# Channel attention on one core: a third buffer for its rows in lent memory, four band buffers, two staging buffers, and one DMA for the rows at a strip edge

## Chip, cores and metric

The kernel runs on one NeuronCore of a Trainium2 chip, in float32 but for one late stage. The metric is the device time of one launch in microseconds (us). The kernel before has a median of 4351.41 us over three runs (4345.83 to 4355.03).

## The reference, cut to what matters

Two layers follow each other on an image batch of shape 4 x 192 x 128 x 128. The first is channel attention with 8 heads of 24 channels, the second a dilated neighbourhood attention. The change lies in the first.

```
# layer 0
qkv = dwconv3x3(conv1x1(x, w_qkv), w_dw)         # 768 channels, 3x3 depthwise, SAME
q, k, v, l = split(qkv, 4)                        # 192 channels each
q, k, v = heads(q), heads(k), heads(v)            # [B, 8, 24, H*W]
q = q / max(norm(q), 1e-12); k likewise           # over all pixels
attn = softmax(einsum("bhcn,bhdn->bhcd", q, k) * temperature)
out = einsum("bhcd,bhdn->bhcn", attn, v)
L = silu(fc2(relu(fc1(mean(l, pixels)))))         # one gate per channel
x = conv1x1(L + out + x, w_proj) + L
# layer 1
x = x + dwconv3x3(x, pos_w) + pos_b
q, k, v = conv1x1(x, qkv_w); attention over 3x3 windows with dilation 1, 2, 3
out = conv1x1(concat, proj_w)
```

## The kernel before, in words

Three stages run one after the other.

`project` (0 to about 820 us) reads x in 64 groups of four rows, multiplies by the 1x1 weights, stores the products for q and k in the DRAM tensor `qk_dram` (laid out row, channel, image, column), and convolves v on DVE, POOL and ACT into `v_dram` and `v2_dram`. A planner (`Schedule`, line 38, wrapped by `Stage`) puts its instructions in order by hand-given costs and places (`PLACES1`), all engines, SP's DMA issues too. Column and row sums for the gate are kept in tiles of `gate_p` (`xsum`, `xcol`, `xrow`, two of each).

`channel_attention` (line 658, about 820 to 1569 us) loops over 8 heads. In each it convolves 24 channels of q and 24 of k on the tensor engine (PE), and forms the products q k^T of each image. Image rows lie on partitions. A 3x3 depthwise convolution becomes, for each column shift dx, a matmul with a banded 32 x 32 matrix over rows; PE is used as sixteen tiles of 32 x 32 (L720), so 24 matmuls make one channel of all four images (6 PSUM buffers `pc`). The work of a head is cut into six turns of 8 channels: q and k, each with j = 0, 2, 4. For each turn `loaded` (L687)
- loads a staging tile `few` of 96 KB with the band's entries (L691, one buffer),
- loads the rows `u` of the 8 channels, 2 MB, by 7 DMAs (L703; the four groups of strips are rotated against each other, so one group takes one DMA and three take two); the pool `u_p` has two buffers,
- builds the turn's band on POOL: four copies of 32 x 720 (L710) and eight of 32 x 6 (L712), into one of two bands, `bands[turn % 2]`.

`evicted` moves a channel from PSUM on ACT (L729) and takes its statistics on DVE (L731). Strips of 32 rows lack the taps that cross their edges. For these, three times a head, `cut_loaded` (L752) loads the four rows around an edge for q and for k (L759: eight DMAs of 48 KB), `cut_convolved` (L766) runs 12 matmuls `pcut` on them after channels 14, 30 and 46, and `cut_turned` (L787) transposes the result (after channels 18 and 34, and inside the gram). `products` (L802) makes the gram of a head, 256 matmuls of 128 x 96 (L807), and small matmuls `sm` (L827 to L845). `finish` (L853) is a generator whose pieces run in the next head after every fourth channel: softmax, two groups of `pm` matmuls with the output weights, and four stores into the tiles `mix1` and `mix2` on SP (L887, L890).

The order on PE is the order of the program text (`manual_schedule(engines={PE})`, L938), with the column shifts of neighbouring channels interleaved. The order on the other engines, SP's queue among them, is set by the framework's scheduler. All of this stage's DMAs are issued by SP, in one queue, and an issue waits there until its target buffer is free.

`second_pass` (L945, 1569 to 4348 us) does layer 1 with the planner again, one iteration per group of four rows of an image pair, 64 in all, about 42.5 us each. Its inputs come in `xv` tiles of 128 x 512 (`loads`, L985; L993 and L996), six per iteration, from a pool `p2xv` of eight buffers that exists from the kernel's start (L337). The products `ph` (L1006) read them. The planner takes the number of buffers from `XV = 8` (`hold`).

The change touches `channel_attention_then_dilated_attention`, `channel_attention`, and in it `loaded`, `cut_loaded`, `products` and `finish`.

Of the kernel before, what the change touches and what calls it, by code (L numbers as in the profile page):

```python
# [7 lines left out]
F32 = mybir.dt.float32  # L8
# [5 lines left out]
B, C, H, W = 4, 192, 128, 128  # L14
HEADS0 = 8
# [22 lines left out]
class Schedule:  # L38
# [6 lines left out]
    def __init__(self, change, change_rank):  # L45
        self.ops, self.pools = [], {}
        self.change, self.change_rank = change, change_rank
# [86 lines left out]
def reached(n, dy):  # L134

    p, i = divmod(n, NB)
    rows = [i * RB + o + dy for o in range(RB)]
    return {p * NB + (-r if r < 0 else 2 * (H - 1) - r if r >= H else r) // RB for r in rows if -4 < r < H + 3}


class Stage:
# [172 lines left out]
@with_exitstack  # L314
def channel_attention_then_dilated_attention(ctx: ExitStack, tc: tile.TileContext, d, out: bass.AP):
    nc = tc.nc
    x = d["x"]
    const = ctx.enter_context(tc.tile_pool(name="const", bufs=1))
    dram = ctx.enter_context(tc.tile_pool(name="dram", bufs=1, space=bass.MemoryType.DRAM))

    def load(pool, name):
        t = pool.tile(list(d[name].shape), d[name].dtype, tag=name, name=name)
        nc.sync.dma_start(t, d[name])
        return t

    mix1, mix2, biases = [], [], []
    for b in range(B):
        mix1.append(const.tile([128, C], F32, tag=f"mix1{b}", name=f"mix1{b}"))
        mix2.append(const.tile([128, C], F32, tag=f"mix2{b}", name=f"mix2{b}"))
    for p in range(B // 2):  # L330
        biases.append(const.tile([128, NG], F32, tag=f"bias{p}", name=f"bias{p}"))
    qk_dram = dram.tile([H, 2 * C, B, W], F32, tag="qk_dram", name="qk_dram")
    v_dram = dram.tile([B // 2, 128, H, 2, W], F32, tag="v_dram", name="v_dram")
    v2_dram = dram.tile([B, G, H, W], F32, tag="v2_dram", name="v2_dram")


    wts2, xv_p = (ctx.enter_context(tc.tile_pool(name=n, bufs=k)) for n, k in (("p2w", 1), ("p2xv", XV)))  # L337
    with ExitStack() as early:
        band_p, u_p = (early.enter_context(tc.tile_pool(name=n, bufs=k)) for n, k in (("pab", 1), ("pau", 2)))
        gate_w = early.enter_context(tc.tile_pool(name="p1g", bufs=1))  # L340
        gate_p = early.enter_context(tc.tile_pool(name="p1s", bufs=2))
        sums = []
        for p in range(B // 2):
            xsum = gate_p.tile([128, 3, NB], F32, tag="xsum", name=f"xsum{p}")
            xcol = gate_p.tile([128, 3, 2, H], F32, tag="xcol", name=f"xcol{p}")
            xrow = gate_p.tile([128, 3, 3], F32, tag="xrow", name=f"xrow{p}")
            nc.gpsimd.memset(xrow, 0.0)
            sums.append((xsum, xcol, xrow))
        later = {}

        def load_later(name, pool):
            later[name] = load(pool, name)

        def load_mix(b):
            nc.sync.dma_start(mix2[b][0:G], d["wp2"])

        loads = [(load_later, n, gate_w) for n in GATE] + [(load_later, n, wts2) for n in SECOND]
        loads += [(load_mix, b) for b in range(B)]
        project(tc, x, load, loads, sums, qk_dram, v_dram, v2_dram)
        gates = [  # L360
            lambda ps, p=p: gate_bias(nc, gate_p, ps, p, *sums[p], *(later[n] for n in GATE), biases[p])
            for p in range(B // 2)
        ]
        channel_attention(tc, d, load, qk_dram, mix1, mix2, band_p, u_p, gates)
        w2 = {n: later[n] for n in SECOND}
    second_pass(tc, x, w2, xv_p, mix1, mix2, biases, v_dram, v2_dram, out)


def project(tc, x, load, other_loads, sums, qk_dram, v_dram, v2_dram):
# [285 lines left out]
    nc.vector.tensor_copy(bias, pb)  # L655


def channel_attention(tc, d, load, qk_dram, mix1, mix2, band_p, u_p, gates):

# [4 lines left out]
    with ExitStack() as ctx:  # L666
# [1 line left out]
        k_p = ctx.enter_context(tc.tile_pool(name="pak", bufs=1))  # L668
        wts = ctx.enter_context(tc.tile_pool(name="paw", bufs=1))
        cut_p = ctx.enter_context(tc.tile_pool(name="pac", bufs=1))  # L670
        few_p = ctx.enter_context(tc.tile_pool(name="pax", bufs=1))
        st = ctx.enter_context(tc.tile_pool(name="pas", bufs=1))
        fin = ctx.enter_context(tc.tile_pool(name="paf", bufs=1))
        ps_c = ctx.enter_context(tc.tile_pool(name="papc", bufs=6, space=bass.MemoryType.PSUM))
# [3 lines left out]
        bands = [band_p.tile([128, 4, 2, 3, STRIP], F32, tag=f"band{k}", name=f"band{k}") for k in range(2)]  # L678
        for band in bands:
            nc.gpsimd.memset(band, 0.0)  # L680
        logits = fin.tile([CH0, B, HEADS0, CH0], F32, tag="logits", name="logits")
        nq = fin.tile([CH0, B, HEADS0], F32, tag="nq", name="nq")
        nk = fin.tile([CH0, B, HEADS0, CH0], F32, tag="nk", name="nk")
        def shifted(dx):
            return slice(max(0, 1 - dx), min(W, W + 1 - dx)), slice(max(0, dx - 1), min(W, W + dx - 1))

        def loaded(hd, which, j):  # L687
# [5 lines left out]
                d["bands"][:, which * C + hd * CH0 : which * C + (hd + 1) * CH0]  # L693
                .rearrange("p (e c) x m -> p e (c x m)", e=4)[:, :, j * 3 * STRIP : (j + 2) * 3 * STRIP],
            )
            u = u_p.tile([128, 4, 2, B * W], F32, tag="u", name=f"u{which}_{hd}_{j}")
            for e in range(4):
                turn = e * STRIP
                for to, of in ((slice(turn, 128), slice(0, 128 - turn)), (slice(0, turn), slice(128 - turn, 128))):
                    if of.start == of.stop:  # L700
                        continue
                    first = c0 + e * (CH0 // 4)
                    nc.sync.dma_start(  # L703
                        u[to, e].rearrange("p c w -> p (c w)"),
                        qk_dram[of, first : first + 2].rearrange("h c b w -> h (c b w)"),
                    )
            band = bands[(3 * (2 * hd + which) + j // 2) % 2]
            for i in range(4):
                group = slice(i * STRIP, (i + 1) * STRIP)
                nc.gpsimd.tensor_copy(band[group, :, :, :, 1 : STRIP - 1], few[:, :, :, :, 1 : STRIP - 1])  # L710
# [41 lines left out]
        def cut_loaded(hd, edge):  # L752
            us = []
            for which in range(2):
                c0 = which * C + hd * CH0
                u = cut_p.tile([4 * CH0, B * W], F32, tag=f"u{which}", name=f"cut{which}_{hd}_{edge}")
                first = (edge + 1) * STRIP - 2
                for r in range(4):
                    nc.sync.dma_start(  # L759
                        u[r * CH0 : (r + 1) * CH0],  # L760
                        qk_dram[first + r, c0 : c0 + CH0].rearrange("c b w -> c (b w)"),
                    )
                us.append(u)
            return us

# [36 lines left out]
        def products(hd, q, sq, k, sk, cuts, s_cut):  # L802
# [43 lines left out]
                    sm[:, 2 * B * CH0 + b : 2 * B * CH0 + b + 1], sq[:, b, :], ones[:, :1], start=True, stop=True  # L846
                )
            by_image = lambda a: a.rearrange("p (b c) -> p b c", b=B)
            nc.vector.tensor_copy(logits[:, :, hd, :], by_image(sm[:, : B * CH0]))
            nc.vector.tensor_copy(nk[:, :, hd, :], by_image(sm[:, B * CH0 : 2 * B * CH0]))  # L850
            nc.vector.tensor_copy(nq[:, :, hd], sm[:, 2 * B * CH0 : EXTRA])

        def finish(hd):  # L853


            rows, norm_q, norm_k = logits[:, :, hd, :], nq[:, :, hd], nk[:, :, hd, :]
            wide = lambda a: a.unsqueeze(2).to_broadcast([CH0, B, CH0])
            for a in (norm_q, norm_k):
                nc.scalar.activation(a, a, AF.Sqrt)
# [18 lines left out]
            for b in range(0, B, 2):  # L878
# [1 line left out]
                pm = ps_g.tile([HALF, B, HALF], F32, tag="gram", name=f"pm{hd}_{b}")  # L880
                two = pm.rearrange("p b c -> p (b c)")[:CH0].rearrange("p (h o) -> p h o", h=2)
                for e in range(2):
                    nc.tensor.matmul(two[:, e, :], logits[:, b + e, hd, :], wph[:, hd, :], start=True, stop=True)
                nc.vector.tensor_copy(mixed, two)
                for e in range(2):
                    if low:
# [694 lines left out]
```

## Time and profile before

| what | value |
|---|---|
| median of three runs | 4351.41 us |
| the profiled execution's own time | 4350.1 us |
| its span, first to last instruction | 4348.2 us |
| granted PE clock, mean | 0.984 |
| busy: PE, DVE, POOL, ACT | 4178.9, 3833.7, 3411.2, 2633.4 us |
| DMA | 676.91 MB, mean 156 GB/s |
| channel attention (820 to 1569 us): PE, DVE, ACT, POOL busy | 689.1, 453.6, 293.9, 236.8 of 749 us |
| its DMA share and rate | 0.63, 160 GB/s |
| projection (100 to 820 us): PE busy, DMA share, rate | 715.1 of 720 us, 0.84, 263 GB/s |
| second pass (1700 to 4000 us): PE, DVE, POOL busy | 2277.7, 2262.1, 2162.8 of 2300 us |
| head 5 (1299 to 1389 us): bytes moved | 14.77 MB |
| head 5: DMA issues on SP | 42 of `u`, 24 of `cut`, 6 of `few`, 2 of `cuttaps`, 4 of `mix` |

Such a page is read like this. "Busy" is time in which an engine executed something; on PE that includes time in which only one of sixteen tiles is at work. The chain of waits is followed back from the last instruction to what released it, step by step. In the table of waits, "A <- B" is time in which engine A stood still with its next instruction at line A, and B came last of what it needed. SPq is the queue of SP: a DMA that stands there holds all behind it.

### The profile page before, as it was taken

The page shows a single profiled execution, that of the slowest core. Times are in us where ns is not written, and L with a number is a line of the kernel's source. Part 1 is how long each engine was busy: PE and PEld are TensorE (multiplying, and loading weights), DVE is VectorE, ACT ScalarE, POOL GpSimd, SP SyncE. Part 2 cuts the span into 40 slices and gives each one's busy share as a digit, 9 for nine tenths or more (in the row PEclk, how much of TensorE's full clock was granted, in tenths as well). Part 3 has the DMA queues.
Part 4 walks back from the last instruction along what each step waited for, and adds up shares of the span by engine and source line. Part 5 has one row for each costly group of instructions (what it writes and reads, how often), then busy time and mean ns, then how long its engine had stood idle before and what let it go on. Part 6 is the DMA issues. An engine that isn't in the chain of part 4 may idle for free.

```text
span 4348.2 us, 74751 instructions
## 1 busy us (share of the span) xinstructions
PE 4178.9 (96%) x25728; PEld 1655.8 (38%) x25728; DVE 3833.7 (88%) x5572; ACT 2633.4 (61%) x4906; POOL 3411.2 (78%) x3409
## 2 busy tenths in 40 slices
PE   8999999899999989999999999999999999999996
PEld 3333333355565543333333333333333333333331
DVE  6999999865656647999999999999999999999996
ACT  6999999733334347565566555665656556566531
POOL 6888888633323315999999999999999999999998
PEclk9999999899999999999999999999999999999997
DMA  8888888766656647566665676656656666665521
GB/s 253 266 267 255 267 273 265 216 168 167 173 137 168 169 109 156 128 135 130 126 129 129 133 130 126 137 116 133 130 126 134 128 129 130 131 136 124 115 50 32
DMA packets 478219, 676.91 MB, mean 156 GB/s; under 512 B 138048, under 2 KB 313612, under 8 KB 477840
## 3 DMA queue, kind: packets, MB, share of 16 engines
q1 hardware_dynamic: 439952, 505.40, 42.7%
q0 software_dynamic: 37888, 166.74, 21.3%
q8 instruction: 204, 3.34, 0.3%
q14 instruction: 175, 1.43, 0.1%
HBM read 278.18 MB, written 201.33 MB: 110 GB/s over the span
## 4 chain that ended last, share of the span: by engine, by line
PE 69%; DVE 13%; DMA 5%; POOL 5%; issue 4%; ACT 2%; SPq 1%; POOLq 0%; DVEq 0%; ACTq 0%
PE sc L1239 9%; PE ex L1361 8%; PE ph L1006 7%; PE pu L414 7%; PE pkv L1160 5%; DVE term L1367 4%; PE pc L720 4%; PE gram L807 4%; PE pkv L1163 4%; PE pu L419 3%; PE q L1217 3%; PE q L1220 3%; DMA u<-qk_dram 3%; DVE prod L1228 3%; POOL acc L1370 3%
## 5 line engine op out<-in xcount | busy, mean ns | idle before, releaser
L1370 POOL TENSOR_TENSOR acc<-acc,term 128x512 f32<-128x512 f32 x1536 | 2036.1, 1331 | 131.3 <-DVE term L1367 44.9
L1367 DVE TENSOR_TENSOR term<-ex,vring 128x512 f32<-128x512 f32 (+2 forms) x1596 | 994.7, 658 | 57.1 <-PE ex L1361 43.8
L1228 DVE TENSOR_TENSOR prod<-q,kring 128x1536 f32<-128x1536 f32 (+1 forms) x600 | 1003.9, 1681 | 19.4 <-PE q L1217 10.1
L491 POOL TENSOR_TENSOR v_True<-v_True,side 128x512 f32<-128x512 f32 (+1 forms) x512 | 643.9, 1270 | 127.8 <-ACT side L480 99.2
L468 DVE SCALAR_TENSOR_TENSOR pa<-vboth,dwv,pa 128x1024 f32<-128x1024 f32 (+1 forms) x448 | 574.2, 1282 | 42.1 <-ACT pa L461 14.0
L1361 PE MATMUL ex<-e_sb,spread 108*128 108x512 bf16 x1728 | 566.9, 386 | 39.7 <-DVE term L1367 32.2
L1173 ACT COPY kring<-pkv 64x512 f32<-64x512 f32 x384 | 223.5, 582 | 417.2 <-PE pkv L1163 411.7
L720 PE MATMUL pc<-u,band 32*32 32x508 f32 (+1 forms) x9216 | 408.2, 611 | 50.1 <-DMA u<-qk_dram 28.8
L1058 DVE SCALAR_TENSOR_TENSOR pa<-hboth,posw,pa 128x1024 f32<-128x1024 f32 (+1 forms) x320 | 407.2, 1273 | 38.0 <-ACT pa L1046 19.1
L712 POOL COPY band<-few 32x6 f32<-32x6 f32 x384 | 78.3, 207 | 448.9 <-DMA few<-in_bands 217.6
L1239 PE MATMUL sc<-prod,pick 128*32 128x512 f32 x3456 | 428.8, 598 | 1.8 <-DVE prod L1228 1.8
L731 DVE BATCH_NORM_STATS2 stats<-conv 128x6 f32<-128x128 f32 x1536 | 313.9, 274 | 129.8 <-ACT conv L729 122.7
L1361 PEld LDWEIGHTS <-spread 108*128 108x128 bf16 x1728 | 133.2, 97 | 650.3 <-issue 627.9
L1006 PE MATMUL ph<-xv,mix 128*64 128x512 f32 (+1 forms) x1024 | 376.1, 598 | 0.5 <-DMA mix<-mixed 0.5
L414 PE MATMUL pu<-xt,wx 128*128 128x512 f32 x768 | 358.2, 609 | 18.3 <-ACT vboth L450 10.4
L1160 PE MATMUL pkv<-y,wkv 128*128 128x512 f32 x768 | 364.3, 596 | 10.7 <-DMA y<-moved 10.5
L1386 ACT COPY o<-po 128x512 f32<-128x512 f32 x192 | 106.3, 588 | 432.1 <-PE po L1383 226.3
L480 ACT ACTIVATE side<-ring,dwv 128x512 f32<-128x512 f32 (+1 forms) x512 | 347.7, 724 | 31.4 <-POOL v_True L491 27.7
L1090 ACT ACTIVATE side<-hring,posw 128x512 f32<-128x512 f32 (+1 forms) x512 | 340.9, 710 | 14.1 <-DMA side<-side 11.9
L729 ACT COPY conv<-pc 128x512 f32<-128x512 f32 x384 | 218.6, 586 | 199.2 <-PE pc L720 187.1
L720 PEld LDWEIGHTS pc<-u,band 32*32 32x32 f32 x9216 | 183.8, 104 | 236.4 <-issue 79.6
L1173 ACT COPY vring<-pkv 64x512 f32<-64x512 f32 x384 | 224.1, 584 | 45.5 <-PE pkv L1163 32.5
(167 smaller groups left out, 6289.9 us busy)
## 6 DMA issues: line engine op xcount, KB each, us to landing
qk_dram<-us SPq DMA_DIRECT2D x192, 512.0 KB
side<-side POOLq DMA_DIRECT2D x124, 768.0 KB, 6.9
u<-qk_dram SPq DMA_DIRECT2D x96, 384.0 KB
xt<-in_x SPq DMA_DIRECT2D x64, 512.0 KB
v_dram<-v_False SPq DMA_DIRECT2D x64, 512.0 KB
xv<-in_x SPq DMA_DIRECT2D x128, 256.0 KB
xv<-v_dram SPq DMA_DIRECT2D x128, 256.0 KB
y<-moved POOLq DMA_DIRECT2D x64, 512.0 KB, 5.2
```

The costliest lines, as they stand in the source:

```text
L414: mm(pu, wx[:, mt * 128 : (mt + 1) * 128], tiles["xt", n][:, im, :], start=True, stop=False)
L468: nc.vector.scalar_tensor_tensor(by_row(to[:, o : o + length]), by_row(vboth[:, at : at + length, :, t % 3 : t % 3 + W]), dwv[:, 0, t : t ...
L491: nc.gpsimd.tensor_add(v[:, rows, :], v[:, rows, :], z[:, rows, :])
L720: nc.tensor.matmul(pc[r * STRIP : (r + 1) * STRIP, :, to], band[at, e, c, dx, :], u[at, e, c, :].rearrange("p (b w) -> p b w", w=W)[:, :, of],
L1006: mm(to, w[:, cols], tiles["xv", n, j, im], start=j == 0, stop=j == 2)
L1160: mm(rows3(tile_of("pc", key)), w, tiles["y", n, im], start=True, stop=False)
L1173: nc.scalar.copy(rows[HALVES[im], :, pad : pad + W], rows3(tiles["pkv", n, pair, im])[HALVES[e]])
L1228: nc.vector.tensor_mul(to[:, :, px].rearrange("p t (r w) -> p t r w", w=W), q.unsqueeze(1).to_broadcast([128, 3, *q.shape[1:]]), three,)
L1239: mm(sc[quad * 32 : (quad + 1) * 32, :], pick[:, QR - 4 * row : QR - 4 * row + 32], tiles["prod", n, k // NT, k % NT // 3][:, k % 3, :], s ...
L1361: mm(rows3(tile_of("ex", ("ex", n, g, t))), spread[:, t, :], e_sb, start=True, stop=True)
L1367: nc.vector.tensor_mul(rows3(to[:, px]), rows3(ex[:, px]), win)
L1370: nc.gpsimd.tensor_add(tiles["acc", n, g], tiles["acc", n, g], tiles.pop(("term", n, g, t)))
```

## The change

- The eight `xv` tiles become one tile `lent` of 128 x 4096 float32. In the channel attention it serves as the third buffer of rows `u`, for the turns with j = 0; the turns with j = 2 and 4 use the two buffers of `u_p` as before. In the second pass a small class `Slices` hands out its eight slices round robin, in the order in which they are asked for.
- Bands: two as before in head 0. When head 1 first loads, two more are taken from the memory of `xcol` in `gate_p` (same size, free once the gate is done) and cleared by POOL. From then on `bands[turn % 4]`.
- `few` gets two buffers.
- The four rows at a strip edge come by one DMA of 192 KB for q and one for k, in place of four of 48 KB each.
- `logits`, `nq` and `nk` keep two heads in place of eight, by `hd % 2`; this makes room and adds no instruction.

In the built program the order of instructions on PE, DVE and ACT is as before. POOL gets the two clearings and its band copies stand in closer groups. On SP the issues of edge rows drop from 192 to 48; the first ten loads of `xv`, which stood at 65 to 93 us, move behind the attention's last read of `lent`; the rows of head 0's third turn stand ahead of the projection's last stores; loads of rows stand about three turns ahead of their use, where they stood two.

```diff
+class Slices:
+    def __init__(self, whole, width):
+        self.whole, self.width, self.given = whole, width, 0
+    def tile(self, shape, dtype, tag, name):
+        at = self.given * self.width % self.whole.shape[1]
+        self.given += 1
+        return self.whole[:, at : at + self.width]
...
-    wts2, xv_p = (ctx.enter_context(tc.tile_pool(name=n, bufs=k)) for n, k in (("p2w", 1), ("p2xv", XV)))
+    wts2, xv_p = (ctx.enter_context(tc.tile_pool(name=n, bufs=1)) for n in ("p2w", "p2xv"))
+    lent = xv_p.tile([128, XV * PX], F32, tag="lent", name="lent")
     with ExitStack() as early:
...
         ]
-        channel_attention(tc, d, load, qk_dram, mix1, mix2, band_p, u_p, gates)
+        channel_attention(tc, d, load, qk_dram, mix1, mix2, band_p, u_p, gate_p, lent, gates)
         w2 = {n: later[n] for n in SECOND}
-    second_pass(tc, x, w2, xv_p, mix1, mix2, biases, v_dram, v2_dram, out)
+    second_pass(tc, x, w2, Slices(lent, PX), mix1, mix2, biases, v_dram, v2_dram, out)
...
-def channel_attention(tc, d, load, qk_dram, mix1, mix2, band_p, u_p, gates):
+def channel_attention(tc, d, load, qk_dram, mix1, mix2, band_p, u_p, gate_p, lent, gates):
...
         cut_p = ctx.enter_context(tc.tile_pool(name="pac", bufs=1))
-        few_p = ctx.enter_context(tc.tile_pool(name="pax", bufs=1))
+        few_p = ctx.enter_context(tc.tile_pool(name="pax", bufs=2))
         st = ctx.enter_context(tc.tile_pool(name="pas", bufs=1))
...
             nc.gpsimd.memset(band, 0.0)
-        logits = fin.tile([CH0, B, HEADS0, CH0], F32, tag="logits", name="logits")
-        nq = fin.tile([CH0, B, HEADS0], F32, tag="nq", name="nq")
-        nk = fin.tile([CH0, B, HEADS0, CH0], F32, tag="nk", name="nk")
+        logits = fin.tile([CH0, B, 2, CH0], F32, tag="logits", name="logits")
+        nq = fin.tile([CH0, B, 2], F32, tag="nq", name="nq")
+        nk = fin.tile([CH0, B, 2, CH0], F32, tag="nk", name="nk")
         def shifted(dx):
...
             )
-            u = u_p.tile([128, 4, 2, B * W], F32, tag="u", name=f"u{which}_{hd}_{j}")
+            turn = 3 * (2 * hd + which) + j // 2
+            if turn % 3 == 0:
+                u = lent.rearrange("p (e c w) -> p e c w", e=4, c=2)
+            else:
+                u = u_p.tile([128, 4, 2, B * W], F32, tag="u", name=f"u{which}_{hd}_{j}")
             for e in range(4):
-                turn = e * STRIP
-                for to, of in ((slice(turn, 128), slice(0, 128 - turn)), (slice(0, turn), slice(128 - turn, 128))):
+                low = e * STRIP
+                for to, of in ((slice(low, 128), slice(0, 128 - low)), (slice(0, low), slice(128 - low, 128))):
                     if of.start == of.stop:
...
                     )
-            band = bands[(3 * (2 * hd + which) + j // 2) % 2]
+            if hd and len(bands) == 2:
+                for k in range(2):
+                    bands.append(gate_p.tile([128, 4, 2, 3, STRIP], F32, tag="xcol", name=f"band{2 + k}"))
+                    nc.gpsimd.memset(bands[-1], 0.0)
+            band = bands[turn % len(bands)]
             for i in range(4):
...
                 first = (edge + 1) * STRIP - 2
-                for r in range(4):
-                    nc.sync.dma_start(
-                        u[r * CH0 : (r + 1) * CH0],
-                        qk_dram[first + r, c0 : c0 + CH0].rearrange("c b w -> c (b w)"),
-                    )
+                nc.sync.dma_start(u, qk_dram[first : first + 4, c0 : c0 + CH0].rearrange("r c b w -> r c (b w)"))
                 us.append(u)
...
             by_image = lambda a: a.rearrange("p (b c) -> p b c", b=B)
-            nc.vector.tensor_copy(logits[:, :, hd, :], by_image(sm[:, : B * CH0]))
-            nc.vector.tensor_copy(nk[:, :, hd, :], by_image(sm[:, B * CH0 : 2 * B * CH0]))
-            nc.vector.tensor_copy(nq[:, :, hd], sm[:, 2 * B * CH0 : EXTRA])
+            nc.vector.tensor_copy(logits[:, :, hd % 2, :], by_image(sm[:, : B * CH0]))
+            nc.vector.tensor_copy(nk[:, :, hd % 2, :], by_image(sm[:, B * CH0 : 2 * B * CH0]))
+            nc.vector.tensor_copy(nq[:, :, hd % 2], sm[:, 2 * B * CH0 : EXTRA])
-            rows, norm_q, norm_k = logits[:, :, hd, :], nq[:, :, hd], nk[:, :, hd, :]
+            rows, norm_q, norm_k = logits[:, :, hd % 2, :], nq[:, :, hd % 2], nk[:, :, hd % 2, :]
             wide = lambda a: a.unsqueeze(2).to_broadcast([CH0, B, CH0])
...
                 for e in range(2):
-                    nc.tensor.matmul(two[:, e, :], logits[:, b + e, hd, :], wph[:, hd, :], start=True, stop=True)
+                    nc.tensor.matmul(two[:, e, :], logits[:, b + e, hd % 2, :], wph[:, hd, :], start=True, stop=True)
                 nc.vector.tensor_copy(mixed, two)
```

## Prediction

> **What bounds the kernel now.** I read the page first. Its table of 40 slices has PE at 9 nearly everywhere and weaker DVE, ACT and POOL digits only in slices 8 to 14, which is the channel attention (820 to 1569 us). The change lies there, so I took that stage's eight heads one by one. From the last matmul of one head (`sm L845`) to the next, heads 1 to 6 take (1481.5 - 935.4)/6 = 91.0 us, head 0 115.4 (820.0 to 935.4), head 7 87.6. Head 5 is 1299.1 to 1389.2, a typical one.
>
> The windows of head 5, for tile `pc` on PE alone, show what "PE busy" hides (columns: window, length, busy and count, granted clock, DMA share, GB/s):
>
> ```profile
> 1303.00:1310.00 7.00, 7.00 (x241) 1.00 0.25 72
> 1317.00:1322.00 5.00, 3.48 (x71) 1.00 0.96 248
> 1326.00:1329.00 3.00, 2.64 (x50) 1.00 0.55 121
> 1333.00:1341.00 8.00, 4.00 (x33) 0.79 0.78 184
> 1348.00:1354.00 6.00, 4.96 (x81) 1.00 1.03 230
> ```
>
> Sixteen 32x32 tiles can be at work at once, so the rate counts, not the busy time. A matmul lasts about 0.6 us and is counted in every window that it touches: 241/(7.0 + 0.6) = 31.7 a microsecond, which is 24/31.7 = 0.757 us for one channel (24 matmuls). In the other windows it is 13, 14, 4 and 12 a microsecond. The chain of waits over the same head says on what:
>
> ```profile
> 1299.08 8.50 PE pc L720 x225
> ...
> 1310.32 8.91 DMA u<-qk_dram
> ...
> 1320.09 7.46 DMA u<-qk_dram
> 1327.60 3.59 PE pc L720 x74
> ...
> 1332.85 0.83 POOL band L710
> ...
> 1346.38 7.71 DMA u<-qk_dram
> 1354.14 5.17 PE pc L720 x129
> 1359.31 2.75 PE pcut L772 x12
> ...
> 1370.08 16.32 PE gram L807 x192
> ```
>
> Three loads of rows (24.1 us) and some POOL work on bands end last while PE creeps. Yet the DMA engines have spare time: share 0.01 in 1299 to 1308, 0.04 in 1374 to 1389. Why the loads come late is in the waits of SP's queue (930 to 1560 us: total, times, longest):
>
> ```profile
> SPq L703 <- PE pc L720: 162.9, 15, 23.6
> SPq L759 <- PE pcut L772: 56.1, 14, 6.1
> SPq L759 <- DMA u<-qk_dram: 49.5, 61, 2.0
> SPq L691 <- POOL band L712: 25.3, 12, 4.4
> ```
>
> With two buffers of rows, the load for turn T can't issue until turn T-2 has been convolved; it then takes 10.9 to 12 us (turn 2 of head 5: 1307.23 to 1319.2), while one turn (8 channels) convolves in 8 x 0.757 = 6.1 us. For 23.6 us at a time, over the whole gram, SP stands still with the third turn of the next head unissued. The bands are in the same state: POOL waits 217.1 us for `pc` (two bands) and 217.6 us for `few` (one staging buffer), overlapping.
>
> **What the Trainium skill says.** "Perfetto Trace Analysis", Optimization Strategy: a gap that repeats on the engine that should be saturated can mean too few buffers. The trace agrees: the creep repeats in every head. "TensorE: Matmul & The Clock Gate", Part 1: an idle window of about 3.4 us halves the clock. The trace has 0.79 granted in 1333 to 1341, just where the convolution starves. "TensorEngine Tiling (Array Packing)", Key Properties: a change of tiling mode drains TensorE; weight loads of `pcut` and `turned` indeed wait up to 0.8 us for it. "DMA: Bandwidth & Descriptors", Why a DMA increments its semaphore by 16 and not by 1: a hardware-issued DMA runs on k engines, the largest k up to 16 that divides the slowest sizes of both sides. No view of the trace of before shows k; I use it below.
>
> **The parts of the change, and their cost.** *Third buffer of rows.* First a head in which nothing is late, on PE, from rows of head 5:
> - 48 channels x 0.757 = 36.3, and 0.9 to get going;
> - three `pcut`: 2.75 each from the chain, 0.8 of drain and 0.35 (estimate) to get going again, 3 x 3.9 = 11.7;
> - two `turned` outside the gram: 0.44 and two half-drains, 2 x 1.45 = 2.9;
> - `pm`: 8 matmuls, 1.6;
> - the last evictions ahead of the gram (1362.13 to 1363.97): 1.8;
> - gram and `sm` (1363.97 to 1389.2): 25.2.
>
> The sum is 80.4. DVE (55.2 busy in that head), ACT (35.4) and POOL (28.3) are below it. DVE alone needs more per channel than PE (39.1/48 = 0.81), but it only reads what ACT has already moved out of PSUM, and its lag of 2 to 3 us is made up under the gram.
>
> Turns end at about 7.0, 16.9, 25.2, 35.2, 42.7 and 52.6 us into the head (6.1 each, plus what stands between). With three buffers, the load for turn T issues when T-3 is done: turn 3 at 7.0, landed by 19, needed at 25.2; turn 4 at 16.9, landed by 29, needed at 35.2; turn 5 at 25.2, held on SP behind the two pairs of `mix` stores to about 30, landed by 41, needed at 42.7. Turns 0 to 2 of the next head issue at 35 to 53 and have landed by about 67: the gram's idle DMA time is used. So 24 us of load stalls shrink to the residue below. What ended last next is PE itself. The head's bytes (14.77 MB) at 235 GB/s take 63 us of DMA, under 80.
>
> *Four bands, two stagings.* The band for turn T can be built once T-4 is done, some 5 us of POOL (4 x 0.795 + 8 x 0.2 = 4.8), 13 us or more ahead of need. This goes with the rows: alone each would leave the other as the bound. The two memsets cost 2 x 0.74 us of POOL once; the first falls in the middle of the projection, the second at 782 to 784 us, where POOL was idle 2.1 us: nothing. Below nothing there is no reason. If the cover were gone: 1.5 us.
>
> *Cut rows by one DMA.* SP issues 18 fewer DMAs a head, each about 0.36 us (the chain's steps of `SPq L759`): 6.5 us off SP's queue, and shorter heads of queue ahead of the `u` loads. But the new source has 4 as its slowest size and the target 96, so by the page k is 4, where 24 and 24 gave 12. An edge's pair (2 x 196.6 KB) then puts 98 KB on each of four engines; at 235/16 = 14.7 GB/s that is 6.7 us. In the new order the pair for edge 1 stands on SP just ahead of turn 4's load: on those four engines turn 4 then lands at 33 to 34 (needed 35.2), and turn 5, behind it, at 43 to 45 (needed 42.7). Their total is (14.77 - 1.18) MB/16 + 6 x 49 KB = 1144 KB a head, 78 us: nearly the bound. If k is not 4 this costs 0, and the issues saved may gain up to 1 us; if 2 KB rows also go slower, 4 us a head. I take 1.6 us of stall a head, which makes it 82.0.
>
> *Lent memory in the second pass.* The eight slots are handed out by index, and some loads (the second of v, the first of the third kind) wait until `ph` of the group is done, at 3028 instead of 3021 in one iteration near 3020. Four loads of 256 KB at the stage's 130 GB/s are 8 us, so they land near 3038; they are needed at about 3049, and the cover is the 11 us that stay. Cost: 0; with the cover gone, each microsecond late costs 62 in the 62 full iterations. The first ten loads (2.05 MB, at 65 to 93 us before) move to the end of the attention, some 9 us of DMA at 235 GB/s, in head 7's gram where the share was low: 0, at worst 3 us if they reach past it.
>
> *The last loads of rows ahead of the projection's end.* Head 0's third turn goes out before the last stores on SP. Turn 1's load stays behind the store of v (issued 838.61, the rows landed 843.2), and DVE's taps to 843 and the gate bound that stretch besides. So head 0 keeps its tail and gains in its later turns only.
>
> **Sum.** Heads 1 to 6: 6 x (91.0 - 82.0) = 54. Head 0: about as one of these, 8.5. Head 7: 87.6 - 82.0 = 5.6. Together 68 us. The profiled execution took 4350.1 us (span 4348.2), so 4282; the median of the runs is 1.3 us higher, which gives 4283.
>
> **Rivals.** *Half of it.* The DMA queues, unevenly loaded, or the convolution's own rate hold the head at 85 to 88 us. For it: the chain's piece of 225 matmuls in 8.50 us is 0.91 us a channel, and 129 in 5.17 is 0.96, above my 0.757; 1144 KB on four engines. Against it: the window with 241. At 86.5: 6 x 4.5 + 5 + 1 = 33 saved, 4318.
>
> *Hidden anyway.* If the bands stayed the bound (POOL waiting as long for `few` as for `pc`), the rows would come early for nothing: about 4347. Against it: staging and bands are doubled too, and POOL is busy 28 of 90 us.
>
> *Slower.* The second pass loses its lead: loads released 7 us later land late on `ph`. For it: PE is busy 99% in 1700 to 4000, so each late load is paid in full. It decides from 11 us of lateness beyond today's; to undo 68 us it must then be late by 68/62 = 1.1 us more in each iteration. At 1.5 us: 4283 + 93 = 4376. Against it: `ph` waited for `xv` not once in the trace of before, and DMA share is only 0.63 there.
>
> **Chances.** The forecast with its own range of 4258 to 4305: 0.60. Half: 0.28. Hidden: 0.05. Slower: 0.07. About 0.2% (9 us) is what a measurement of this kernel can tell from no change. Faster: 0.88; same 0.05; slower 0.07. The range of 4258 to 4325 takes in most of the half case and leaves out the last two and little beside. Its low end is a head of about 79: no skew on four engines, and my 80.4 too high by 1.4.
>
> **What would show it.** The heads at 80 to 84 us; in the chain of a head `pc`, `gram` and `pcut` with `u<-qk_dram` below 8%; SP's longest wait at the gram gone; DMA busy under the gram; `pc` at about 30 a microsecond in every turn. If turn 5 (or 4) still waits for `u`, the cut DMAs on few engines or the `mix` stores are the cause. Wrong would be: heads above 86, a wait of `ph` for `xv`, or a longer second pass than 2779 us (1569 to 4348).

## The result, and the profile after

The changed kernel took 4380.06 us (median of four runs, 4374.27 to 4391.09), the kernel before 4348.68 beside it: a ratio of 1.0073, interval 1.005 to 1.0097. It is slower, by 31 us; 4283 was forecast. The profiled execution took 4374.27 us, with a span of 4372.3. Cut at the same instructions (the last `sm` matmul of each head), the two spans stand so:

| us | before | after | difference | forecast |
|---|---|---|---|---|
| start to the end of head 0 | 935.4 | 952.0 | +16.6 | -8.5 |
| heads 1 to 6 | 546.1 (91.0 each) | 543.1 (90.5 each) | -3.0 | -54 |
| head 7 | 89.7 | 86.7 | -3.0 | -5.6 |
| the rest, the second pass | 2777.0 | 2790.5 | +13.5 | 0 |
| span | 4348.2 | 4372.3 | +24.1 | -68 |

So the convolution's heads hardly gained, head 0 lost, and the second pass lost. The chain of waits of the changed kernel over head 5 (1312.4 to 1403.2), start, length, what:

```profile
1312.37 11.66 PE pc L741 x314
...
1343.08 2.31 issue
1345.39 3.24 PE pc L741 x74
...
1355.34 4.39 PE pc L741 x119
1359.73 13.46 DMA cut<-qk_dram
```

The three pieces for rows `u` (24 us before) are gone, as forecast. In their place stands one of 13.46 us for the edge rows of the third edge. Such a piece runs from the issue of a load to its landing (here 1359.73 to 1373.19); it is not the time for which PE stood. PE's own timeline shows that (start, length, instruction, in brackets the idle time before it):

```profile
1355.27 6.71 PE L741 MATMUL pc<-u,band 32*32 32x512 f32 x191
1366.12 5.87 PE L741 MATMUL pc<-u,band 32*32 32x508 f32 x89 [4.14 <-issue]
1371.92 1.06 PE L789 MATMUL pcut<-cut,cuttaps 96*48 96x512 f32 x2
1373.24 2.76 PE L789 MATMUL pcut<-cut,cuttaps 96*48 96x512 f32 x10 [0.26 <-DMA cut<-qk_dram]
```

PE stands 4.14 us with nothing in view to wait for ("issue"), then convolves four channels slowly (the granted clock is 0.50 from 1366 to 1370), and then waits about 1 us for the edge rows. Without that stall it would most likely have waited for them the longer. PE's waits over heads 1 to 6 (952.0 to 1495.1; total, times, longest):

```profile
PE pc L741 <- issue: 32.3, 18, 4.1
PE pcut L789 <- DMA cut<-qk_dram: 11.7, 6, 3.6
PE pc L741 <- DMA u<-qk_dram: 1.2, 2, 0.9
```

In the kernel before (935.4 to 1481.5) they were:

```profile
PE pc L720 <- DMA u<-qk_dram: 18.1, 28, 1.6
PE pc L720 <- issue: 1.4, 2, 0.8
```

PE's windows of `pc` in head 5 show the slow stretch: 0.74 of the clock and 146 matmuls in 13 us.

```profile
1312.00:1319.00 7.00, 6.70 (x199) 1.00 0.01 2
1360.00:1373.00 13.00, 7.85 (x146) 0.74 1.05 211
```

In the waits of SP's queue (930 to 1560 us), the wait for `pc` is cut into 47 pieces where it was 15. New are 81 us in which SP stands until a load `cut` has landed (0.4 us before). In this trace SP's DMAs use eight completion semaphores in turn, and an issue waits until the load eight issues earlier has landed (the one at 1373.21 went out 0.02 us after the landing at 1373.19), so a late edge load also holds the bulk loads behind it on SP.

```profile
SPq L720 <- PE pc L741: 139.1, 47, 20.8
SPq L704 <- DMA cut<-qk_dram: 41.5, 13, 4.0
SPq L720 <- DMA cut<-qk_dram: 39.7, 24, 3.7
SPq L779 <- PE pcut L789: 36.4, 7, 7.3
```

### The profile page after: what moved, and what is told of

Read it like the earlier page. It is cut to its first block, busy times and chain, and to the rows that moved or that the text cites. A ratio compares the mean times of both kernels' runs of the same rounds, so it can differ in the third digit from the quotient of the medians.

```text
span 4372.3 us, 74543 instructions
## 1 busy us (share of the span) xinstructions
PE 4159.7 (95%) x25728; PEld 1669.8 (38%) x25728; DVE 3818.5 (87%) x5572; ACT 2632.4 (60%) x4906; POOL 3407.6 (78%) x3411
## 3 DMA queue, kind: packets, MB, share of 16 engines
q0 software_dynamic: 37888, 166.74, 20.6%
## 4 chain that ended last, share of the span: by engine, by line
PE 71%; DVE 14%; DMA 5%; issue 5%; POOL 3%; ACT 2%; SPq 1%; DVEq 0%; POOLq 0%; ACTq 0%
PE sc L1256 9%; PE ex L1378 8%; PE ph L1023 8%; PE pu L427 6%; PE pkv L1177 5%; PE pc L741 5%; DVE term L1384 4%; PE gram L824 4%; PE pkv L1180 4%; PE q L1237 4%; PE q L1234 4%; PE pu L432 3%; DVE prod L1245 3%; PE po L1400 2%; PE pu L578 2%
## 5 line engine op out<-in xcount | busy, mean ns | idle before, releaser
L1023 PE MATMUL ph<-lent,mix 128*64 128x512 f32 (+1 forms) x1024 | 375.5, 598 | 1.8 <-DMA mix<-mixed 1.8
L1403 ACT COPY o<-po 128x512 f32<-128x512 f32 x192 | 106.3, 588 | 446.2 <-PE po L1400 240.0
L1107 ACT ACTIVATE side<-hring,posw 128x512 f32<-128x512 f32 (+1 forms) x512 | 341.7, 713 | 11.7 <-DMA side<-side 9.8
L741 PE MATMUL pc<-u,band 32*32 32x508 f32 (+1 forms) x6144 | 281.3, 624 | 36.6 <-issue 22.1
L1190 ACT COPY vring<-pkv 64x512 f32<-64x512 f32 x384 | 224.3, 584 | 45.5 <-PE pkv L1180 32.6
L427 PEld LDWEIGHTS pu<-xt,wx 128*128 128x128 f32 x768 | 143.1, 193 | 225.6 <-issue 122.3
```

What stands on the lines that cost most here:

```text
L427: mm(pu, wx[:, mt * 128 : (mt + 1) * 128], tiles["xt", n][:, im, :], start=True, stop=False)
L741: nc.tensor.matmul(pc[r * STRIP : (r + 1) * STRIP, :, to], band[at, e, c, dx, :], u[at, e, c, :].rearrange("p (b w) -> p b w", w=W)[:, :, of],
L1023: mm(to, w[:, cols], tiles["xv", n, j, im], start=j == 0, stop=j == 2)
L1190: nc.scalar.copy(rows[HALVES[im], :, pad : pad + W], rows3(tiles["pkv", n, pair, im])[HALVES[e]])
```

## The experiments

Fourteen kernels ran. Times are medians, ratios are to the kernel before on the same chip; lengths of heads come from the one profiled execution of each.

### Edge rows by four DMAs again, and the second pass's own pool

In `cut4` only the edge rows' edit is undone:

```diff
-                nc.sync.dma_start(u, qk_dram[first : first + 4, c0 : c0 + CH0].rearrange("r c b w -> r c (b w)"))
+                for r in range(4):
+                    nc.sync.dma_start(
+                        u[r * CH0 : (r + 1) * CH0],
+                        qk_dram[first + r, c0 : c0 + CH0].rearrange("c b w -> c (b w)"),
+                    )
```

> The changed kernel with the edge rows loaded by four DMAs of 48 KB again (that edit alone undone). Theory A (a merged load of 4 x 24 rows runs on few DMA engines, so the pair lands late and holds what is queued behind it on those engines): the 13.5 us wait for cut in each head's chain falls below 4 us, heads 1 to 7 take 82 to 84 us instead of 90, the time falls by 40 to 55 us, to about 4330. Rival B (three turns of rows are issued ahead, and a small load that is issued late lands behind them however it is cut): the wait for cut stays at 11 to 13 us, heads stay at 89 to 91, the time stays within 10 us of 4380.

Measured: 4323.91 us, ratio 0.9954 (0.9937 to 0.9971). Heads 1 to 6 take 83.5 us, 7.0 less each. The chain of head 5 (1271.7 to 1356.7) has, up to its third `pcut`, PE alone in it but for short stalls put down to "issue":

```profile
1300.03 2.05 issue
...
1305.48 2.70 PE pcut L793 x12
...
1312.19 6.36 PE pc L741 x163
1318.55 2.50 issue
1321.05 5.80 PE pc L741 x104
1326.85 2.75 PE pcut L793 x12
```

The third `pcut` follows the convolution at once, and over heads 1 to 6 PE waits for `cut` not at all. Theory A holds; the one DMA per edge was the cost.

`pool` gives the second pass a pool of its own again, and so undoes the slots by index alone:

```diff
-    lent = xv_p.tile([128, XV * PX], F32, tag="lent", name="lent")
     with ExitStack() as early:
+        xv_p = early.enter_context(tc.tile_pool(name="pal", bufs=1))
+        lent = xv_p.tile([128, XV * PX], F32, tag="lent", name="lent")
...
-            dict(xv=xv_p),
+            {},
```

> The changed kernel, but the lent tile is given back at the end of the attention and the second pass has a pool of eight xv tiles of its own again, which hands out whichever tile is free. Theory C (slots handed out by index make SP's queue stand for one slot with a transposing load for the softmax weights behind it, once near 1748 us for 12.6 us): second pass 2777 us as in the kernel before instead of 2790, time down by 11 to 15 us, to about 4367. Rival (that wait comes from the later start of the first loads, which stays): within 3 us of 4380.

Measured: 4351.89 us, ratio 1.0019 (1.001 to 1.0027), 28 us under the changed kernel, where 11 to 15 were expected. The profiled executions differ by 13.0 (4372.3 and 4359.3), and in that of `pool` the second pass takes 2773.1 us, 17 less. Theory C holds; why the medians differ by more is open. SP's queue shows the place, first in the kernel before (start, length, instruction, times):

```profile
1733.25 1.43 SPq L993 DMA_DIRECT2D xv<-in_x  x2
1737.22 1.45 SPq L1326 DMA_TRANSPOSE e_sb<-parts  x1
```

and in the changed kernel, whose attention ends 10.7 us later:

```profile
1725.37 17.79 SPq L1010 DMA_DIRECT2D lent<-v_dram  x2
1743.21 1.10 SPq L1013 DMA_DIRECT2D lent<-in_x  x1
...
1748.33 4.39 SPq L1343 DMA_TRANSPOSE e_sb<-parts  x1
```

The second of two loads of v stands for its slot (17.79 us from the first's start to the second's end), and six loads wait behind it. They go out within 4.2 us, and directly behind them the transposing load of the softmax weights. Counted from the attention's end this load is issued at 166.5 us, where it was 166.1 before, so its issue is not late. It lands late: 19.6 us after its issue, where it is 6.3 in the kernel before and in `pool`. PE waits for it:

```profile
PE ex L1378 <- DMA e_sb<-parts: 13.1, 2, 12.6
```

Once, for 12.6 us, near the start of the second pass; later iterations show no such wait.

`cut4_pool` joins both edits.

> Both edits together. If A and C both hold and are independent: about 4380 - 48 - 13 = 4319. If only C: 4367. If neither: 4380. Head 0 should still be long (about 130 us from 820), if its loss comes from the order of POOL's band copies and not from the edge rows; under A alone it would fall to about 115 too.

Measured: 4311.7 us, ratio 0.9921 (0.99 to 0.9941), heads 83.9, second pass 2772.7. The two gains do not quite add up: 56 and 28 us alone, 68 together (64, 13 and 71 in the profiled executions). Head 0 stays long (its end at 945.5), as expected if its loss is POOL's.

`before_merged` is the kernel before with the one DMA per edge, the first diff above the other way round.

> The kernel before with the one edit that loads an edge's four rows by one DMA. Theory A: rows u land later behind it, heads grow by 3 to 6 us each, the time grows by 25 to 45 us, to 4375 to 4395. Rival B: 18 fewer issues a head on SP, nothing else, the time falls by 0 to 8 us, to 4341 to 4349.

Measured: 4385.6 us, ratio 1.0096 (1.0074 to 1.0118). Heads 1 to 6 take 95.2 us, 4.2 more. Here PE never waits for `cut` itself; it is the rows behind that come later. PE's waits for them in heads 1 to 6, 18.1 us before, are now:

```profile
PE pc L720 <- DMA u<-qk_dram: 44.3, 20, 4.4
```

Its chain over head 4 (1227.2 to 1321.6):

```profile
1244.95 9.91 DMA u<-qk_dram
...
1271.84 10.94 DMA u<-qk_dram
```

So this edit alone costs 40 us (4345.2 beside it) in a kernel that has nothing else of the change, though it takes 144 issues off SP.

### The load by itself

`loads_alone` leaves all of the work out and times the forms of the load:

```diff
+    nc.sync.dma_start(u, rows[r1 : r1 + r, : c * 512].rearrange("r (c w) -> r c w", w=512))
```

> A kernel that leaves all of the work out and only times loads of 96 x 512 float32 into one tile (and pairs of them), one after the other, nothing else on the DMA engines: four DMAs of 24 rows; one DMA with a source of 4 x 24 rows, as in the change; one of 16 x 6; one of 2 x 48; one of 96 plain rows. The output is not the reference's. Theory A with its rule (as many engines as divide both slowest sizes, up to 16: 12, 4, 16, 2, 16): a pair of 4 x 24 takes about 4 to 7 us more than a pair of 16 x 6, a pair of 2 x 48 about twice the excess again, plain rows the same as 16 x 6, four DMAs of 24 between. Rival (one DMA of this size costs the same whatever its source's sizes; the loss in the kernel came from its place in the queue): all forms within 1 us.

DVE copies a column of each tile as soon as it has landed. Its timeline in one round (a form is timed as one single load and then as a pair; of two forms only the pair is shown; start, length, instruction):

```profile
55.43 0.15 DVE L344 COPY seen<-rfour 96x1 f32<-96x1 f32 x1 [3.19 <-DMA rfour<-in_x]
60.41 0.15 DVE L344 COPY seen<-rfour 96x1 f32<-96x1 f32 x1 [4.83 <-DMA rfour<-in_x]
62.31 0.15 DVE L344 COPY seen<-rfour 96x1 f32<-96x1 f32 x1 [1.75 <-DMA rfour<-in_x]
66.73 0.15 DVE L344 COPY seen<-rsixteen 96x1 f32<-96x1 f32 x1 [3.11 <-DMA rsixteen<-in_x]
67.23 0.15 DVE L344 COPY seen<-rsixteen 96x1 f32<-96x1 f32 x1 [0.35 <-DMA rsixteen<-in_x]
80.44 0.15 DVE L344 COPY seen<-rtwo 96x1 f32<-96x1 f32 x1 [6.82 <-DMA rtwo<-in_x]
84.38 0.15 DVE L344 COPY seen<-rtwo 96x1 f32<-96x1 f32 x1 [3.78 <-DMA rtwo<-in_x]
```

What the second load of a pair adds is close to its transfer alone: 1.90 us for 4 x 24, 0.50 for 16 x 6, 3.94 for 2 x 48. With 196.6 KB each this is 103, 393 and 50 KB a microsecond, and divided by 4, 16 and 2 engines it is 25.9, 24.6 and 25.0 for one engine. (For 16 x 6 SP itself takes 0.6 us between the two issues, so there the figure is rough.) Windows with only such loads in them show the engines in another way: the busy share of the sixteen is 0.25 for 4 x 24 and 0.12 for 2 x 48, and 0.78 for 16 x 6 (columns: window, length, DVE and POOL busy, clock, DMA share, GB/s).

```profile
53.20:54.80 1.60, 0.00 (x0) 0.00 (x0) 1.00 0.25 93
68.80:72.80 4.00, 0.00 (x0) 0.00 (x0) 1.00 0.12 44
65.30:66.50 1.20, 0.00 (x0) 0.00 (x0) 1.00 0.78 278
```

So the engines used are 4, 2 and 16, as the Trainium skill, "DMA: Bandwidth & Descriptors", Why a DMA increments its semaphore by 16 and not by 1, has it: the largest number up to 16 that divides the slowest sizes of both sides. The pair as the change has it takes 6.7 us from its release, as 16 x 6 it takes 3.6; the excess of 3.1 is less than the 4 to 7 expected. The rival (all forms alike) is out.

The same is seen inside the kernels. A trace also keeps, though no view prints it, when each DMA engine reports its part of a load as landed. From 940 us to the end of the attention, all 40 merged edge loads of the changed kernel end with four such reports, all 160 loads of `cut4` with twelve (one update about 1 us after the issue, which comes besides where fewer than sixteen engines are used, is left out). Each of the 120 loads of rows issued within 8 us after a merged edge load has four or five of its sixteen engines more than 2 us behind its median engine, and its last engine is 5.8 us behind it in the median. In `cut4` none of the 152 such loads has more than three, and the last engine is 1.5 us behind. So the four engines, with the edge rows queued first, do hold up the rows behind them.

### What head 0 waits for

In head 0 of the changed kernel POOL's timeline reads so:

```profile
878.83 0.70 POOL L733 COPY band<-few 32x6 f32<-32x6 f32 x2
897.03 0.77 POOL L731 COPY band<-few 32x720 f32<-32x720 f32 x1 [17.50 <-DMA few<-in_bands]
...
904.18 0.78 POOL L731 COPY band<-few 32x720 f32<-32x720 f32 x1 [1.88 <-DMA few<-in_bands]
...
908.98 3.28 POOL L731 COPY band<-few 32x720 f32<-32x720 f32 x4
```

and PE's, for head 0's last turn:

```profile
910.64 11.45 PE L741 MATMUL pc<-u,band 32*32 32x512 f32 x208 [13.23 <-POOL band L731]
```

POOL waits 17.5 us for the staging load of turn 4. Then the built program has copies for bands 2 and 3, which head 1 needs, among those for turn 5, and the one for band 3 waits again, for a staging load just issued. The four large copies of turn 5 come last, at 909, and PE stands for 13.2 us. `pool_order` writes POOL's order out:

```diff
-        with tc.manual_schedule(engines={mybir.EngineType.PE}):
+        with tc.manual_schedule(engines={mybir.EngineType.PE, mybir.EngineType.Pool}):
```

> Four DMAs for the edge rows and a pool of its own for the second pass, as in cut4_pool, and besides POOL's order in the attention written out as PE's is (the order of the program text). Theory D (head 0 is long because POOL's copies for the new bands of head 1 stand ahead of those for head 0's last turn and wait for their staging loads): head 0 ends near 930 instead of 945.3, heads 1 to 7 stay at 84, the time falls by 12 to 17 us, from 4312 to about 4298. Rival (the staging loads themselves are late in the DMA queues, whatever POOL's order): within 4 us of 4312.

Measured: 4303.24 us, ratio 0.9895 (0.9869 to 0.992), 8.5 under `cut4_pool`, where 12 to 17 were expected. The two ratios' intervals overlap, so the times alone do not settle it; the length of head 0 does. Counted from POOL's last sum of the projection, head 0 takes 98.7 us, `cut4_pool` 106.3, the changed kernel 111.8, the kernel before 96.8. So of 15 us lost in head 0 some 7.6 are POOL's order and 5.5 go with the two edits of `cut4_pool`. Theory D holds with a smaller share than stated. The edge rows have a share of their own here: in `before_merged`, which has no new bands, head 0 takes 105.0 us.

### Rows, bands, staging: which of them brings the gain

`rows2` keeps two buffers of rows, with the rest of the change, four DMAs for the edges and the pool. `bands2` keeps two bands. `rows3_only` keeps two bands and one staging buffer, and so is the third buffer alone.

```diff
-            if turn % 3 == 0:
+            if False:
```

> As cut4_pool, but with two buffers of rows throughout (the lent tile is left unused). If the third buffer brings the gain: heads 1 to 6 back at 89 to 91 us, the time 4350 to 4360. If the bands and the staging alone brought it: heads 84 to 85, 4312 to 4320.

Measured: 4337.55 us, ratio 0.9981 (0.9973 to 0.9988), heads 88.0. The third buffer is worth 4.1 us a head against `cut4_pool`. The bands and the staging without it are worth 3.0 (91.0 to 88.0), which neither branch of the expectation had.

```diff
-            if hd and len(bands) == 2:
+            if False:
```

> As cut4_pool, but with two bands throughout. If the bands bound as well, as the prediction had it (rows early for nothing without them): heads 1 to 6 fall back from 84 to 88 to 90 us, 4345. If the rows were the only bound: heads stay at 84. Head 0 has no new bands to build in its midst: it ends near 930 and not at 945, so 4298 in that case.

Measured: 4304.51 us, ratio 0.9895 (0.9864 to 0.9927), heads 84.3. With the third buffer there, two more bands bring 0.4 us a head at most. Head 0 takes 97.4 us from the projection's last sum.

```diff
-        few_p = ctx.enter_context(tc.tile_pool(name="pax", bufs=2))
+        few_p = ctx.enter_context(tc.tile_pool(name="pax", bufs=1))
```

> The kernel before with the third buffer of rows alone (four DMAs for the edges, two bands, one staging buffer, a pool of its own for the second pass). If staging and bands are needed to use the third buffer: heads 1 to 6 at 87 to 90 us, 4325 to 4345. If rows alone were the bound: 84, about 4305, as with two bands and two staging buffers.

Measured: 4303.7 us, ratio 0.9899 (0.9875 to 0.9923), heads 84.6, head 0 96.1. Rows alone bring 6.4 us a head, and bands and staging add 0.7 to that.

### What is left in a head

`ordered_cutbuf` gives the edge rows two buffers each, and the staging tile one.

```diff
-                u = cut_p.tile([4 * CH0, B * W], F32, tag=f"u{which}", name=f"cut{which}_{hd}_{edge}")
+                u = cut_p.tile([4 * CH0, B * W], F32, tag=f"u{which}{(3 * hd + edge) % 2}", name=f"cut{which}_{hd}_{edge}")
```

> As pool_order, and each edge-row tile has two buffers, so that the third edge's loads are issued two turns earlier; the staging tile goes back to one buffer to make room. Theory B in part (what is left of the wait for cut, 5 to 7 us a head, is that the loads are issued behind two turns of rows): that wait goes, heads 1 to 7 take 79 to 81 us, 25 us less than pool_order: about 4273. Rival (the DMA engines are just full then, and rows are late instead; or the single staging buffer blocks): heads stay at 83 to 85, within 5 us of pool_order.

Measured: 4301.85 us, ratio 0.989 (0.9868 to 0.9913), heads 83.4. No gain over `pool_order` that could be told: the rival holds, earlier edge rows are worth nothing once they come by four DMAs.

`mix_on_act` and `cutbuf_mix_on_act` issue the stores of the output weights from ACT, with two buffers for their source:

```diff
-                        nc.sync.dma_start(mix1[b + e][hd * CH0 : hd * CH0 + low], mixed[:low, e, :])
+                        nc.scalar.dma_start(mix1[b + e][hd * CH0 : hd * CH0 + low], mixed[:low, e, :])
```

> As pool_order, but the four stores of the output weights per head are issued by ACT in place of SP and their source has two buffers. If those stores hold the load of turn 5 on SP's queue, as the prediction had it (turn 5 landing after its need): the stall of 3 to 4 us before turn 5 goes, heads 1 to 6 take 80 to 81 us and not 84.1, the time falls from 4303 to about 4280. Rival (the DMA engines are full there anyway, or ACT's evictions are held by the issues): heads stay at 83 to 85.

> As ordered_cutbuf, with the same edit. If the edge rows' lead then counts as well: heads 79 to 80, about 4275. If not: as mix_on_act within 3 us, or worse by the single staging buffer.

Measured: 4314.64 us, ratio 0.9918 (0.9898 to 0.9938), and 4319.72, ratio 0.9936 (0.9918 to 0.9954), heads 85.4 and 86.3 (84.1 and 83.4 without the edit). The second is worse than `ordered_cutbuf` beyond the intervals; those of the first and `pool_order` overlap. The chain of `mix_on_act` in head 4 says why:

```profile
1225.04 0.73 ACTq L909
...
1226.43 1.54 DVE stats L753 x8
...
1229.62 0.45 DVE mixed L906
...
1231.56 0.73 ACTq L909
...
1232.39 0.59 ACT conv L751
```

ACT stands with the second pair of stores until DVE has copied their source; DVE has its statistics ahead of that copy; the evictions behind on ACT wait, and PE for them. The test did not answer its question, so two more leave the stores on SP and only double their source:

```diff
-                mixed = fin.tile([CH0, 2, C], F32, tag="mixed", name=f"mixed{hd}_{b}")
+                mixed = fin.tile([CH0, 2, C], F32, tag=f"mixed{b}", name=f"mixed{hd}_{b}")
```

> As pool_order, with two buffers for the source of the output-weight stores, which stay on SP. If the second pair of stores holds turn 5's load on SP until the first pair has landed (4 to 6 us): that wait goes, the stall before turn 5 shrinks from 3.4 us to under 1, heads 1 to 6 take 81 to 82.5 us, the time falls by 10 to 18 us, from 4303 to about 4289. Rival (the DMA engines are full while turns 3 to 5 are loaded, so turn 5 lands late anyway): heads stay at 83.5 to 84.5, within 4 us of 4303.

> The same edit on rows3_only. As above: if the stores hold the loads, from 84.6 to about 82.5 a head and from 4304 to about 4290; if the DMA engines are full, 4304.

Measured: 4303.4 us, ratio 0.9905 (0.9889 to 0.9922), and 4302.35, ratio 0.9899 (0.9882 to 0.9915). In the profiled execution of `order_mixed2` heads take 82.6 us and the stall before turn 5 of the head from 1184.5 is 1.77 us, where `pool_order` had 3.37; its median is that of `pool_order`. Inconclusive for heads, no gain in the time.

The traces point to another cause of that stall than the stores. In `pool_order` it ends at 1235.29 with no releaser in view ("issue"), and so do 143 idle pieces of PE of 0.4 us or more in heads 1 to 6 of the fifteen kernels (all but `loads_alone`). Among the DMA packets of these stretches are some of another kind than loads. The changed kernel's stall of 4.14 us has one (1362.5 to 1366; queue, kind, packets, MB, share):

```profile
q8 instruction: 1, 0.02, 2.4%
```

There are 72 of these 16 KB packets in the six heads of the changed kernel, one for each 250 of PE's matmuls and weight loads. Every one of the 143 stalls ends 1.3 to 1.8 us after the end of such a packet. So PE had most likely run out of instructions there, and neither rows nor stores held it. No run changed the fetching, so this is read from the traces and not tested. The stalls take 1.4 us in six heads before, 32.6 in the changed kernel, 20.6 in `cut4`, 25.1 in `pool_order` and 7.3 in `rows3_only`.

Six versions lie within 3 us of each other at 4302 to 4305 us and beat the kernel before by about 1%: `pool_order`, `ordered_cutbuf`, `bands2`, `rows3_only` and the two above. The plainest is `rows3_only`.

## Why the prediction was wrong

*The load stalls on rows.* Right. "24 us of load stalls shrink to the residue": PE's waits for `u` in heads 1 to 6 fall from 18.1 to 1.2 us, and the third buffer alone brings heads from 91.0 to 84.6 us. But the 24 us a head were pieces from issue to landing, in which PE went on creeping; they were not there to be gained in full.

*"I take 1.6 us of stall a head"* for the edge rows. This step failed, by size: the term is worth 7.0 us a head (90.5 against 83.5 in `cut4`). Its first links were right: four engines, the place on SP, and the lag of the rows behind a pair (6.7 us computed, 5.8 in the median in the trace). But I made a stall of it only where turns 4 and 5 land, and PE does not stall there. It stalls in three other places. It waits for the edge rows themselves, 11.7 us in six heads and 0 in `cut4`; the third edge, which I never followed, is issued at 1358.24 and 1359.73, behind turn 5 and five of the seven loads of the next turn 0, and lands at 1373.19. It stands 12 us longer than in `cut4` in the stalls put down to "issue". And its matmuls run more slowly (PE busy 488.3 us in six heads against 470.6), in part at the halved clock after such a stall. Together that is about the 42 us. That the four engines cause it is shown by `cut4`, `before_merged` and `loads_alone`; how they lead to the second and third of these is open. SP's 81 us behind edge loads are a likely link.

I also took 78 us of work on four engines as just under a bound of 80. With the stretch of 7 us in which the DMA share is 0.01 (1312 to 1319) it is 85, by an estimate at 14.7 KB a microsecond; that this bound was reached is not shown.

*"If k is not 4 this costs 0, and the issues saved may gain up to 1 us".* The issues saved gained nothing that shows: in `before_merged` they are all there, and the kernel is 0.96% slower.

*"This goes with the rows: alone each would leave the other as the bound."* Wrong. The rows alone bring 6.4 us a head, and the bands and staging alone 3.0. POOL's 217 us of waiting for `pc` and for `few` are no measure of it: with the third buffer there, two bands take 84.6 and 84.3 us a head and four 83.9.

*The new bands cost "nothing", at most 1.5 us.* Wrong. The two clearings were hidden, but the order of POOL's copies around them was not looked at in time: 7 to 8 us in head 0.

*"Head 0: about as one of these, 8.5".* Wrong even without those losses: 96.1 us in `rows3_only` against 96.8 before. Why the third buffer brings nothing there is open; I did not try it.

*The second pass: "Cost: 0".* Wrong by 13.5 us in the profiled executions, 12 (`cut4_pool` against `cut4`) to 28 (`pool` against the changed kernel) in medians. I asked what `ph` waits for, and that was right: `ph` never waited for rows. I did not ask what follows a waiting load on SP: six loads in a burst, and behind them the transposing load. The rival that ended slower had the place, but not the mechanism: it is one stall at the start, not one per iteration.

*A head without stalls, 80.4.* Not contradicted. With four DMAs heads are 83.4 to 84.6, but in `cut4` 3.4 us a head of that are stalls put down to "issue", and one head of `order_mixed2` (1184.5 to 1263.9), with one such stall of 1.77, takes 79.4. The parts of the sum were less right: the first 361 matmuls of a head in `pool_order` take 13.46 us, 0.89 us a channel, and not 0.757, which is the rate of the best 7 us.

*Head 7, 87.6.* Misread: that ends with the first of the closing matmuls; to the last `sm` at 1571.1 it is 89.7.

The errors are of one sign: 51 us in heads 1 to 6, 25 in head 0, 2.6 in head 7 and 13.5 in the second pass make the 92 us between 4282 and 4374.3.

## What to carry to other kernels

Fewer DMA issues are no gain when the merged pattern has a small slowest size: look at the slowest sizes of both sides, and at what the few engines then hold up behind them. Follow each small urgent load to its need, the last one too. When buffers are handed out in another way, ask of every wait on the issuing queue what stands behind it and goes out in a burst when it ends. Take a piece `DMA x` in the chain as time from issue to landing, and ask the engine's own waits how long it stood. And where a stall is put down to "issue", look for packets of the kind `instruction` before changing the loads or stores around it.

## What the runs showed of the hardware that was not expected

The forms of the 196.6 KB load in `loads_alone` move 24.6 to 25.9 KB a microsecond for each engine used, with 2, 4 and 16 engines alike, where the rows `u` in the kernel run at about 14.7 (235 GB/s over 16). So it is not the number of engines that makes the difference; what in the kernel does is open. A load on four engines with nothing beside it takes 1.9 us and not the 3.3 that 14.7 would give; alone the skew would be a smaller loss than in the kernel.

A transposing load of the softmax weights that directly followed six bulk loads took 19.6 us from issue to landing, where it took 6.3 at the same place in the kernel before (over all 64 of these loads the median is 4.1 there, the longest 16.0). The bulk loads had landed by 1754.1, 13.9 us before it; what held it after that is open. And PE, when its data come early enough, stands for its own instructions: 32.6 us in six heads of the changed kernel, if the reading above is right.
